# Hypergraph layer beside a state-space layer: norm chain, row norms and edge sums issued in separate, later steps

## The chip, the cores and the metric

The kernel runs on one core of a Trainium2 chip. Time is device time in microseconds (us). Engines are named as in the profile: PE does matmuls (PEld its weight loads), DVE is the vector engine, ACT the scalar engine, POOL is GpSimd, SP issues most of the DMAs. SBUF is the on-chip memory of 128 partitions; PSUM holds what PE writes[...].

## The reference

Four layers act on four images of 128 channels and 64 x 64 = 4096 points. Layer 0 is a Mamba-like scan over the points. Layer 1 is a hypergraph convolution on the group-normalized result. Layers 2 and 3, linear attention and experts, are not touched by the change. Layer 1, for one image, with `xf` the points as 4096 rows of 128 numbers:

```python
sq = jnp.sum(xf * xf, axis=-1)
d2 = sq[:, :, None] + sq[:, None, :] - 2.0 * jnp.einsum('bic,bjc->bij', xf, xf)
incidence = (jnp.sqrt(jnp.maximum(d2, 0.0)) < 16.0)
xe = jnp.einsum('bnc,dc->bnd', xf, W_fc) + b_fc
edge = jnp.einsum('bve,bvc->bec', incidence, xe) / deg_e
vert = jnp.einsum('bve,bec->bvc', incidence, edge) / deg_v
out = vert + xf        # then batch norm and SiLU, added to the layer's input
```

Layer 0's core is `h = dA * h + (dt * x) * B` for 16 states of 256 channels, point after point, and `y = sum(h * C)`.

## The kernel before, in words

`layers01` writes layers 0 and 1 as two Python generators and interleaves them. `layer0` works in chunks of 512 points, 8 per image, with 16 states per chunk. A state is two half-steps: ACT takes two exponentials into a PSUM tile (`hs`, L303), DVE scans both channel halves (L309), copies the carry (L318) and multiplies by C (`ho`, L319), POOL multiplies the drive (`db`, L291) and adds up eight states (`ho_s`, L324 and L326), PE sums into `ps_y` (L347) once a chunk. SP loads the rows B and C for each state (`bt`, L287). An image has 256 half-steps. Layer 0 runs 12 half-steps ahead (`LAG`).

`layer1(b)` is one image of the hypergraph. Its steps are: a prologue that turns the channel statistics of layer 0 into `rstd` and `nmr` (a matmul with `group` for the mean, `ps_gm`; a chain of one-column DVE operations L449 to L452; a second matmul `ps_gv`; a square root on ACT, L455; a reciprocal and a product on DVE), eight loads of `xn` and their normalization on ACT (L463); `tokens(q)`, which for 512 points takes squares on ACT (L468), their sums on PE (`ps_hc`), and `xe` with its split into two float16 parts in `xs`; then for each chunk c of 512 edges, from 7 down to 0, `compare` for the tiles up to c (PE `ps_g`, L504, and DVE `inc`, L507) and `turn` for the others, which gets them by transposing what is there (PE `ps_t`, L516, and ACT, L520). Rows of `inc` go to DRAM and come back as `strip` and `inc_v` by SP's queue. `row(c)` makes the row norm `hb` that `compare` of chunk c needs: a square on ACT, a matmul with ones (`ps_hb`, L495), a scaling on DVE (L497). `edges(inc, ed, c, i)` runs 32 matmuls into one PSUM tile (`ps_ed`, L527) that holds two parts of 129 columns each; ACT copies the first part to SBUF (L533) and DVE adds the second (L534). After four of them DVE, POOL and ACT divide by the degree and split `es` (L538 to L545). At the end, eight times, PE sums the vertices (`ps_v`, L627), `mean` scales on DVE (`rb`, L635) and adds `xn` on POOL (L636), and `finish` takes statistics on DVE (L639) and stores to DRAM (`hg`, L640).

The order comes from three things. `later(k, f)` puts a closure into `waiting`; `due()` runs it k ticks on. While layer 0 runs, a tick is one half-step of it. A planner gives each yield of `layer1` a weight (`W_CMP`, `W_EDGE` and so on) and, after each half-step, advances `layer1` until its share of the whole `work` is done. In the last image, with no layer 0 left, every yield is a tick. ACT's instructions are tied to the order in which they are written (`act`); the other engines' come from a scheduler that orders by priority and by when buffers come free.

The pools that matter: `ps` has four PSUM banks for all matmul results of both layers but `hs`; `tp` (squares and `xe` under one tag, `hb` and `dg`, `rb`, `inc`, `strip`) has two buffers for each tag; `xn` has one for each chunk.

```python
later(1, parts)     # in edges
later(1, mean)      # after the eighth group of vertex matmuls
later(4, finish)
```

Of the kernel before, what the change touches and what calls it, by code (L numbers as in the profile page):

```python
# [17 lines left out]
P = 128  # L18
# [23 lines left out]
class Net:  # L42
# [36 lines left out]
    def layers01(self):  # L79
# [6 lines left out]

        W_ROW, W_TOK, W_CMP, W_TURN, W_EDGE, W_LAST, W_DEG, W_VERT = 300, 450, 320, 75, 100, 630, 160, 267
        G = 8
        TO_POOL = (1, 4, 6, 9, 12, 14)
        LAG = 6 * 2  # L90
        with ExitStack() as ctx:
# [110 lines left out]
            def later(k, f):  # L202
                waiting.append((self.tick + k, f))
# [234 lines left out]

            def layer1(b):

                mv = tp.tile([P, 2], F32, tag="mv", name="mv")
                nc.vector.bn_aggr(mv, self.stats[:, b, :, :].rearrange("p c s -> p (c s)"))
# [4 lines left out]
                pg = ps.tile([P, CH], F32, tag="ps", name="ps_gm")  # L447
                nc.tensor.matmul(pg[:, :1], self.group, mv[:, 0:1], start=True, stop=True)
                nc.vector.tensor_copy(gm, pg[:, :1])  # L449
                nc.vector.tensor_tensor(nmr, mv[:, 0:1], gm, ALU.subtract)  # L450
                nc.vector.tensor_tensor(nmr, nmr, nmr, ALU.mult)
                nc.vector.tensor_tensor(nmr, nmr, mv[:, 1:2], ALU.add)  # L452
                pg = ps.tile([P, CH], F32, tag="ps", name="ps_gv")
                nc.tensor.matmul(pg[:, :1], self.group, nmr, start=True, stop=True)
                act(nc.scalar.activation(rstd, pg[:, :1], AF.Sqrt, bias=self.eps))  # L455
                nc.vector.reciprocal(rstd, rstd)
                nc.vector.scalar_tensor_tensor(nmr, gm, -1.0, rstd, ALU.mult, ALU.mult)

                xn = []
                for c in range(NCH):  # L460
                    x = wp.tile([P, CH], F32, tag=f"xn{c}", name="xn")
                    nc.sync.dma_start(x, self.x1[b][:, c * CH : (c + 1) * CH])
                    act(nc.scalar.activation(x, x, AF.Identity, scale=rstd, bias=nmr))  # L463
                    xn.append(x)

                def squares(c):
# [24 lines left out]

                def row(c):

                    ph = ps.tile([P, CH], F32, tag="ps", name="ps_hb")
                    nc.tensor.matmul(ph, self.ones, squares(c), start=True, stop=True)  # L495
                    hb = tp.tile([P, CH], F32, tag="hb", name="hb")
                    nc.vector.tensor_scalar(hb, ph, 0.5, -HALF, ALU.mult, ALU.add)  # L497
                    return hb

# [22 lines left out]
                def edges(inc, ed, c, i):  # L522
# [9 lines left out]
                    def parts():  # L532
                        act(nc.scalar.copy(ed[:, i, :], pe[:, : P + 1]))  # L533
                        nc.vector.tensor_tensor(ed[:, i, :], pe[:, P + 1 : 2 * P + 2], ed[:, i, :], ALU.add)  # L534
                        if i == 3:
# [10 lines left out]

                    later(1, parts)


                panels = [None] * NCH  # L550
                last = None
                hb = row(NCH - 1)
                yield W_ROW
                for c in range(NCH - 1, -2, -1):
# [6 lines left out]
                    for q in range(8):  # L561
                        if c == NCH - 1:
                            tokens(q)
                            yield W_TOK
                        if 0 <= c < q:
                            src = last[0][:, 4 * c : 4 * c + 4, :]
# [10 lines left out]
                        if c > 1:  # L577
# [5 lines left out]
                            )  # L583
                        if q == 6 and c > 0:
                            ahead = row(c - 1)
                            yield W_ROW
                        if last and q % 2:
# [3 lines left out]
                            yield W_EDGE if c >= 0 else W_LAST  # L591
                    hb = ahead
                    last = (inc, ed)
# [15 lines left out]
                for c in range(NCH):  # L609
# [39 lines left out]
            work = NCH * (W_ROW + W_TOK + W_DEG + 8 * W_VERT) + 4 * (NCH - 1) * W_EDGE + 4 * W_LAST  # L649
# [3 lines left out]
            for _ in range(states + LAG):  # L653
                next(l0)
            for b in range(B):
                l1 = layer1(b)
                if b < B - 1:
                    done = 0
                    for k in range(states):
                        next(l0, None)  # L660
                        self.tick += 1
                        due()
                        while done * states < work * (k + 1):
                            done += next(l1)
                else:
# [844 lines left out]
```

## Time and profile before

| | |
|---|---|
| median of 3 runs | 4132.1 us (4127.52 to 4135.44) |
| the profiled execution | 4130.31 us, span 4128.5 us |
| mean granted PE clock | 0.919 |
| busy share of the span | PE 84%, PEld 47%, DVE 72%, ACT 50%, POOL 60% |
| layer 0 of image 0 alone | to about 568 us |
| three passes, layer 0 of image b+1 beside layer 1 of image b | about 775, 775 and 763 us |
| layer 1 of image 3 alone | from about 2881 us |

The profile takes one execution with the hardware profiler. Its page lists busy time for each engine, the span in slices, the chain that ended last, and the costliest groups of instructions. Asked further, the trace lists who waited for whom, instructions in order of time, and busy time in chosen stretches. A wait is put down to what came last. In a line of a group or of the timeline, `out<-in` are the program's tile names, and the bracket or the last column tells how long the engine stood idle before it and what released it.

### The profile page before, as it was taken

How to read it: one execution, taken by the hardware profiler on the slowest of the kernel's cores; microseconds unless marked ns; L12 is line 12 of the kernel's file. 1: busy time of each engine (PE TensorE's matmuls, PEld its weight loads, DVE VectorE, ACT ScalarE, POOL GpSimd, SP SyncE). 2: the span in 40 equal slices, each digit the busy share in tenths (PEclk: the TensorE clock that was granted, in tenths of full speed). 3: DMA queues.
4: the chain of work that ended last, by engine and by line, in shares of the span. 5: the costliest groups of instructions: out<-in, count | busy, mean ns of one | idle time of the engine just before them, and what ended most of it. 6: DMA issues, size and time to landing. Idle time of an engine off the chain costs nothing. (4 is left out here: it accounts for less than half of the span.)

```text
span 4128.5 us, 48675 instructions
## 1 busy us (share of the span) xinstructions
PE 3469.8 (84%) x17243; PEld 1944.5 (47%) x17255; DVE 2990.9 (72%) x4628; ACT 2065.6 (50%) x3495; POOL 2460.4 (60%) x1242
## 2 busy tenths in 40 slices
PE   6878767888889688888977888888999979998999
PEld 2323323344543334445333344543566448765864
DVE  5888879999766799976669999765542057664874
ACT  4556554445644544555444445642124148852951
POOL 5999879888778788877869888775100020001300
PEclk8988977899999788999987899999999989999999
DMA  3445544555446344543644555447111330036138
GB/s 106 146 146 153 155 110 123 133 135 153 128 127 196 105 131 131 139 138 102 206 130 125 133 135 152 127 127 236 70 69 60 115 111 11 12 117 239 27 107 297
DMA packets 263847, 532.71 MB, mean 129 GB/s; under 512 B 22795, under 2 KB 25267, under 8 KB 262579
## 3 DMA queue, kind: packets, MB, share of 16 engines
q1 hardware_dynamic: 255666, 519.09, 43.1%
q10 hardware_dynamic: 7936, 10.52, 0.7%
q8 instruction: 136, 2.23, 0.2%
q14 instruction: 109, 0.89, 0.1%
HBM read 451.80 MB, written 77.73 MB: 128 GB/s over the span
## 5 line engine op out<-in xcount | busy, mean ns | idle before, releaser
L291 POOL TENSOR_TENSOR db<-dx,bt 128x1024 f32<-128x1024 f32 x512 | 1202.6, 2352 | 330.9 <-DVE hs L309 216.4
L309 DVE TENSOR_TENSOR_SCAN hs<-hs,carry,db 128x512 f32<-128x512 f32 x812 | 1037.2, 1285 | 174.6 <-ACT hs L303 91.8
L303 ACT ACTIVATE hs<-dl,A 128x512 f32<-128x512 f32 x1024 | 706.7, 692 | 750.2 <-DVE ho L319 696.8
L326 POOL TENSOR_TENSOR ho_s<-ho_s,ho 128x1024 f32<-128x1024 f32 x288 | 677.5, 2352 | 17.4 <-DVE ho L319 16.7
L504 PE MATMUL ps_g<-xn 128*128 128x512 f32 x1152 | 603.7, 654 | 99.8 <-DVE inc L507 74.8
L319 DVE TENSOR_TENSOR ho<-hs,bt 128x1024 f32<-128x1024 f32 x464 | 564.6, 1217 | 1.6
L527 PE MATMUL ps_ed<-xs,inc 128*128 128x258 f16 x4096 | 510.7, 285 | 19.1 <-ACT inc L520 8.6
L527 PEld LDWEIGHTS <-inc 128*128 128x128 fp8e4 x4096 | 416.3, 102 | 135.0 <-issue 62.4
L507 DVE SCALAR_TENSOR_TENSOR inc<-ps_g,hcl,hb 128x512 fp8e4<-128x512 f32 x576 | 422.0, 739 | 40.0 <-PE ps_g L504 24.4
L504 PEld LDWEIGHTS ps_g<-xn 128*128 128x128 f32 x1152 | 216.4, 205 | 417.5 <-DVE inc L507 184.1
L347 PE MATMUL ps_y<-ho,cst 128*128 128x512 f32 x512 | 276.3, 683 | 109.5 <-POOL ho L315 92.2
L627 PE MATMUL ps_v<-inc_v,es 128*128 128x512 fp8e4 x1536 | 342.9, 382 | 19.7 <-DVE rb L635 9.4
L627 PEld LDWEIGHTS <-es 128*128 128x128 f16 x2048 | 202.4, 99 | 289.5 <-issue 64.4
L520 ACT CAST inc<-ps_t 128x512 fp8e4<-128x512 f32 x448 | 232.2, 599 | 94.6 <-PE ps_t L516 94.6
L229 PE MATMUL ps_c<-xt,wc 128*128 128x512 f32 x512 | 231.3, 605 | 11.1 <-DVE inc L507 6.8
L347 PEld LDWEIGHTS ps_y<-ho,cst 128*128 128x128 f32 x512 | 106.2, 217 | 271.4 <-POOL ho L315 122.7
L533 ACT COPY ed<-ps_ed 128x129 f32<-128x129 f32 x128 | 34.1, 266 | 378.8 <-PE ps_ed L527 378.8
L534 DVE TENSOR_TENSOR ed<-ps_ed,ed 128x129 f32<-128x129 f32 x128 | 36.8, 288 | 211.2 <-ACT ed L533 208.1
L543 POOL TENSOR_TENSOR ed<-ed,rdeg 128x512 f32<-128x512 f32 x32 | 33.3, 1040 | 250.0 <-DVE rdeg L539 250.0
L1179 POOL CAST b1h<-b 128x512 bf16<-128x512 f32 x2 | 1.3, 649 | 299.7 <-DMA b<-in_L_ffn_weight 299.7
L309 DVE TENSOR_TENSOR_SCAN hs<-hs,db 128x512 f32<-128x512 f32 x116 | 141.4, 1225 | 52.9 <-POOL db L291 41.9
L229 PEld LDWEIGHTS ps_c<-xt,wc 128*128 128x128 f32 x512 | 98.2, 195 | 135.1 <-issue 115.9
(318 smaller groups left out, 5485.4 us busy)
## 6 DMA issues: line engine op xcount, KB each, us to landing
bt<-bcd SPq DMA_DIRECT2D x512, 512.0 KB, 5.1
w<-in_L_ffn_weight SPq DMA_DIRECT2D x64, 1024.0 KB, 11.4
inc<-inc SPq DMA_DIRECT2D x192, 256.0 KB, 2.8
inc_v<-inc SPq DMA_DIRECT2D x96, 512.0 KB, 6.3
strip<-inc SPq DMA_DIRECT2D x84, 256.0 KB, 4.8
x<-x ACTq DMA_DIRECT2D x32, 256.0 KB, 5.6
xn<-x SPq DMA_DIRECT2D x32, 256.0 KB, 5.6
hg<-rb SPq DMA_DIRECT2D x32, 256.0 KB, 2.6
```

The source lines that it names most:

```text
L229: nc.tensor.matmul(s["ps"][h], wc[:, h, j, :], xt[:, j : j + T], start=j == 0, stop=j == 3)
L291: nc.gpsimd.tensor_tensor(db, s["dx"], bc(s["bt", n][:, 0, :], 2), ALU.mult)
L303: act(nc.scalar.activation(hs[:, k, :], s["dl"][:, k, :], AF.Exp, scale=A[:, k, n : n + 1]))
L309: nc.vector.tensor_tensor_scan(to[:, h, :], hs[:, h, :], db[:, h, :], init, ALU.mult, ALU.add)
L319: nc.vector.tensor_tensor(ho, hs, ct, ALU.mult)
L326: nc.gpsimd.tensor_tensor(s["sum", n // G], s["sum", n // G], ho, ALU.add)
L347: nc.tensor.matmul(s["y"][h], self.ident, t[:, h, :], start=False, stop=n == DS - 1 and k == len(terms) - 1,)
L504: nc.tensor.matmul(pq, xn[v // 4][:, v % 4 * P : (v % 4 + 1) * P], xn[c], start=True, stop=True)
L507: nc.vector.scalar_tensor_tensor(inc[:, v, :], pq, hc[:, v : v + 1], hb, ALU.subtract, ALU.is_gt, saturate=False)
L520: later(1, lambda: act(nc.scalar.copy(inc[:, v, :], pt, saturate=False)))
L527: nc.tensor.matmul(pe[:, : 2 * P + 2], inc[:, v, i * P : (i + 1) * P], xs[:, v, :], start=v == 0, stop=v == NB - 1,)
L627: nc.tensor.matmul(pv, es[:, e, k, :], inc[:, e, :], start=e == 0 and k == 0, stop=e == NB - 1 and k == 1,)
```

## The change

- The prologue becomes a function of its own with four steps: means, variances, root, shift. The first three are written in the last three half-steps of layer 0 before the pass, the fourth at its start.
- `layer1` issues its eight `xn` loads in its first step. `normed(c)` normalizes chunk c and squares it. Chunk 7 and chunk 0 are done first; `tokens(q)` is given its squares, and `normed(q + 1)` is written behind it.
- `row(c)` is split into square, sum (2 ticks on) and scaling (3 ticks on), is written at q = 4 instead of 6 for all chunks but the first, and gives back a function that finishes what is left.
- `parts` adds both parts of an edge tile straight from PSUM with one DVE reduction over a view of 129 x 2, without ACT's copy, 2 ticks on instead of 1.
- `finish` comes 6 ticks on instead of 4.
- The planner's weights get `W_PRO` for the two new yields.

```diff
-            def layer1(b):
-                mv = tp.tile([P, 2], F32, tag="mv", name="mv")
-                nc.vector.bn_aggr(mv, ...)
...
+            def prologue(b):
...
+                def means():
+                    nc.vector.bn_aggr(mv, self.stats[:, b, :, :].rearrange("p c s -> p (c s)"))
+                    s["pg"] = ps.tile([P, CH], F32, tag="ps", name="ps_gm")
+                    nc.tensor.matmul(s["pg"][:, :1], self.group, mv[:, 0:1], start=True, stop=True)
+                def variances():
+                    nc.vector.tensor_copy(gm, s["pg"][:, :1])
...
+                def root():
+                    act(nc.scalar.activation(rstd, s["pg"][:, :1], AF.Sqrt, bias=self.eps))
+                def shift():
+                    nc.vector.reciprocal(rstd, rstd)
+                    nc.vector.scalar_tensor_tensor(nmr, gm, -1.0, rstd, ALU.mult, ALU.mult)
+                return rstd, nmr, [means, variances, root, shift]
+            def layer1(b, rstd, nmr):
                 for c in range(NCH):
                     x = wp.tile([P, CH], F32, tag=f"xn{c}", name="xn")
                     nc.sync.dma_start(x, self.x1[b][:, c * CH : (c + 1) * CH])
-                    act(nc.scalar.activation(x, x, AF.Identity, scale=rstd, bias=nmr))
                     xn.append(x)
+                yield W_PRO
...
+                def normed(c):
+                    act(nc.scalar.activation(xn[c], xn[c], AF.Identity, scale=rstd, bias=nmr))
+                    return squares(c)
-                def tokens(c):
-                    sq = squares(c)
+                def tokens(c, sq):
...
-                def row(c):
-                    ph = ps.tile([P, CH], F32, tag="ps", name="ps_hb")
-                    nc.tensor.matmul(ph, self.ones, squares(c), start=True, stop=True)
-                    hb = tp.tile([P, CH], F32, tag="hb", name="hb")
-                    nc.vector.tensor_scalar(hb, ph, 0.5, -HALF, ALU.mult, ALU.add)
-                    return hb
+                def row(c, sq=None):
...
+                    if sq is None:
+                        s["sq"] = squares(c)
+                        later(2, step)
+                        later(3, step)
+                    return get
...
                     def parts():
-                        act(nc.scalar.copy(ed[:, i, :], pe[:, : P + 1]))
-                        nc.vector.tensor_tensor(ed[:, i, :], pe[:, P + 1 : 2 * P + 2], ed[:, i, :], ALU.add)
+                        both = pe[:, : 2 * P + 2].rearrange("p (k c) -> p c k", k=2)
+                        nc.vector.reduce_sum(ed[:, i, :], both, axis=AX.X)
...
-                    later(1, parts)
+                    later(2, parts)
...
-                hb = row(NCH - 1)
-                yield W_ROW
+                hb = row(NCH - 1, normed(NCH - 1))
+                sq = normed(0)
+                yield W_PRO
...
-                            tokens(q)
+                            if q == 0:
+                                hb = hb()
+                            tokens(q, sq)
                             yield W_TOK
+                            if q < NCH - 2:
+                                sq = normed(q + 1)
+                            elif q == NCH - 2:
+                                sq = squares(q + 1)
...
-                        if q == 6 and c > 0:
+                        if q == (4 if c < NCH - 1 else 6) and c > 0:
                             ahead = row(c - 1)
...
-                    later(4, finish)
+                    later(6, finish)
```

More of the change, by code (lines that the diff above doesn't have):

```diff
@@ L84, in layers01 @@
         TOP = 2.0**14
-        W_ROW, W_TOK, W_CMP, W_TURN, W_EDGE, W_LAST, W_DEG, W_VERT = 300, 450, 320, 75, 100, 630, 160, 267
+        W_PRO, W_ROW, W_TOK, W_CMP, W_TURN, W_EDGE, W_LAST, W_DEG, W_VERT = 330, 300, 450, 320, 75, 100, 630, 160, 267
         G = 8
@@ L437, in layers01 @@
             stats = wp.tile([P, B, NCH, 6], F32, tag="stats1", name="stats1")
-            def layer1(b):
-                mv = tp.tile([P, 2], F32, tag="mv", name="mv")
-                nc.vector.bn_aggr(mv, self.stats[:, b, :, :].rearrange("p c s -> p (c s)"))
+            def prologue(b):
                 gm = tp.tile([P, 1], F32, tag="gm", name="gm")
@@ L446, in layer1 @@
                 nmr = tp.tile([P, 1], F32, tag="nmr", name="nmr")
[L447 to L457, printed above, removed]
+                mv = tp.tile([P, 2], F32, tag="mv", name="mv")
+                s = {}
+                def means():
[4 more added lines that the diff above has]
+                    nc.vector.tensor_copy(gm, s["pg"][:, :1])
+                    nc.vector.tensor_tensor(nmr, mv[:, 0:1], gm, ALU.subtract)
+                    nc.vector.tensor_tensor(nmr, nmr, nmr, ALU.mult)
+                    nc.vector.tensor_tensor(nmr, nmr, mv[:, 1:2], ALU.add)
+                    s["pg"] = ps.tile([P, CH], F32, tag="ps", name="ps_gv")
+                    nc.tensor.matmul(s["pg"][:, :1], self.group, nmr, start=True, stop=True)
+                def root():
[5 more added lines that the diff above has]
+            def layer1(b, rstd, nmr):
                 xn = []
@@ L490, in tokens, with sums, half, step @@
                     later(3, lambda: nc.gpsimd.tensor_tensor(lo, xe, hi, ALU.subtract))
-                def row(c):
-                    ph = ps.tile([P, CH], F32, tag="ps", name="ps_hb")
-                    nc.tensor.matmul(ph, self.ones, squares(c), start=True, stop=True)
-                    hb = tp.tile([P, CH], F32, tag="hb", name="hb")
-                    nc.vector.tensor_scalar(hb, ph, 0.5, -HALF, ALU.mult, ALU.add)
-                    return hb
+                def row(c, sq=None):
+                    s = dict(sq=sq)
+                    def sums():
+                        s["ph"] = ps.tile([P, CH], F32, tag="ps", name="ps_hb")
+                        nc.tensor.matmul(s["ph"], self.ones, s["sq"], start=True, stop=True)
+                    def half():
+                        s["hb"] = tp.tile([P, CH], F32, tag="hb", name="hb")
+                        nc.vector.tensor_scalar(s["hb"], s["ph"], 0.5, -HALF, ALU.mult, ALU.add)
+                    steps = [sums, half]
+                    def step():
+                        if steps:
+                            steps.pop(0)()
+                    def get():
+                        while steps:
+                            step()
+                        return s["hb"]
+                    if sq is None:
[3 more added lines that the diff above has]
+                    return get
                 def compare(inc, hb, c, v):
@@ L591, in layer1 @@
                             yield W_EDGE if c >= 0 else W_LAST
-                    hb = ahead
+                    if c > 0:
+                        hb = ahead()
                     last = (inc, ed)
@@ L643, in layer1 @@
                     later(1, mean)
-                    later(4, finish)
+                    later(6, finish)
                 while waiting:
                     due(True)
-            work = NCH * (W_ROW + W_TOK + W_DEG + 8 * W_VERT) + 4 * (NCH - 1) * W_EDGE + 4 * W_LAST
+            work = 2 * W_PRO - W_ROW + NCH * (W_ROW + W_TOK + W_DEG + 8 * W_VERT) + 4 * (NCH - 1) * W_EDGE + 4 * W_LAST
             work += NCH * (NCH + 1) // 2 * 4 * W_CMP + NCH * (NCH - 1) // 2 * 4 * W_TURN
@@ L652, in layers01 @@
             l0 = layer0()
-            for _ in range(states + LAG):
+            norm = prologue(0)
+            for k in range(states + LAG):
                 next(l0)
+                if k >= states + LAG - 3:
+                    norm[2].pop(0)()
             for b in range(B):
-                l1 = layer1(b)
+                norm[2].pop(0)()
+                l1 = layer1(b, *norm[:2])
                 if b < B - 1:
+                    norm = prologue(b + 1)
                     done = 0
@@ L664, in layers01 @@
                             done += next(l1)
+                        if k >= states - 3:
+                            norm[2].pop(0)()
                 else:
```

## The prediction

> **What bounds the kernel now.** The page gives PE 84%, DVE 72%, POOL 60%, averages over unlike stages. I cut the span into stages by busy time. Layer 0 of image 0 runs alone to 568 us, three passes (layer 0 of image b+1 beside the hypergraph of image b) run to 2881, the hypergraph of image 3 runs alone to about 3200, and the rest is untouched. Columns: length, then busy us of PE, PE weight loads, DVE, ACT, POOL, then granted clock, DMA share, GB/s. The first four rows are one pass: norm, compares, turns with edges, vertices.
>
> ```profile
> 568.00:595.00 27.00, 7.64 (x24) 5.92 (x25) 16.88 (x22) 16.44 (x23) 16.12 (x7) 0.50 0.30 78
> 595.00:1015.00 420.00, 350.20 (x1302) 176.98 (x1301) 388.57 (x499) 214.29 (x317) 371.44 (x169) 0.89 0.50 132
> 1015.00:1165.00 150.00, 127.02 (x847) 83.29 (x845) 100.80 (x128) 92.02 (x158) 104.55 (x49) 0.93 0.42 115
> 1165.00:1345.00 180.00, 157.68 (x620) 68.97 (x618) 123.04 (x127) 79.00 (x129) 147.42 (x69) 0.93 0.63 183
> ...
> 2881.00:3190.00 309.00, 279.58 (x1719) 184.30 (x1717) 132.55 (x214) 82.79 (x169) 23.24 (x21) 0.96 0.21 77
> ```
>
> No engine is full in a pass. DVE leads in the compares (31 us idle of 420), PE in turns and vertices (23 of 150 and 22 of 180 idle). So a DVE wait is worth about its length in the compares, and no more than PE's own idle time later. The last row is PE's. Next, the list of waits of DVE over the three passes: total us, times, longest.
>
> ```profile
> DVE stats L639 <- POOL rb L636: 103.7, 21, 8.9
> DVE hs L309 <- ACT hs L303: 101.3, 51, 5.2
> DVE ed L534 <- ACT ed L533: 75.8, 30, 7.8
> DVE hb L497 <- PE ps_hb L495: 59.8, 15, 8.6
> DVE hs L309 <- POOL db L291: 36.2, 32, 1.9
> ```
>
> The first, third and fourth are aimed at. The second hangs on them: ACT works in order, so an edge copy that waits for PE holds the exponentials of layer 0 behind it. Last, the timeline at the first prologue:
>
> ```profile
> 577.24 0.58 PE L454 MATMUL ps_gv<-nmr,cst 128*128 128x1 f32 x2 [8.58 <-DVE nmr L452]
> 577.86 0.26 ACT L455 ACTIVATE rstd<-ps_gv,eps 128x1 f32<-128x1 f32 x1 [3.36 <-PE ps_gv L454]
> ...
> 582.07 5.75 ACT L463 ACTIVATE xn<-xn,nmr,rstd 128x512 f32<-128x512 f32 x8 [3.94 <-DVE nmr L457]
> 587.85 1.15 ACT L468 ACTIVATE sq<-xn 128x512 f32<-128x512 f32 x2
> 588.53 0.50 PEld L495 LDWEIGHTS ps_hb<-sq,ones 128*128 128x128 f32 x2 [10.79 <-ACT sq L468]
> ...
> 590.64 0.69 DVE L497 TENSOR_SCALAR hb<-ps_hb 128x512 f32<-128x512 f32 x1 [8.61 <-PE ps_hb L495]
> ```
>
> Eight normalizations stand between the shift and the first square; PE and DVE wait for all of them. Layer 0's exponentials are queued behind.
>
> **What the Trainium skill says.** "VectorE: DVE Perf Modes" (The perf-mode tier table) has `tensor_reduce` in its 1x form alone. The trace agrees: 278 ns for 128 elements read and 553 for 384 is 1.07 ns an element. "SBUF — State Buffer" (SBUF: two separate sides) says a DVE operation with two SBUF inputs and a GpSimd operation exclude each other for a whole instruction. It agrees: the one-column `nmr` steps of L450 to L452 took 1.12, 1.18 and 2.26 us beside POOL's. Spreading the chain doesn't make them cheap. "TensorE: Matmul & The Clock Gate" (Part 1) has the clock fall after idle windows: 0.50 in the first row against 0.89 after it.
>
> **The change part by part.** The order of instructions in the two built programs tells what moves.
>
> *Prologue, four times.* The chain is emitted in the last three half-steps before the pass, but on DVE in passes 2 and 3 it stands back to back, with no scan between. What does change: the reciprocal now follows the variance directly (PE 0.58, ACT 0.26, about 1 us of wait as at the second prologue before), and ACT does normed(7), its square, normed(0), its square, not eight normalizations first. First pass: root ends 578.1; table load 1.28 and two exponentials 1.42 make 580.8; one normalization 0.80 and one square 0.63 make 582.2; PE's row sum 2.08 makes 584.3 for `hb` in place of 590.6: 6.3 gained with the same DVE work ahead of it. In passes 2 and 3 a new wait appears: chunk 7 is wanted first now, and its buffer is the last to come free, by the old pass's `rb` on POOL. I put that at 1350.5, the load at 2.4 to 5.6 us (a store of `rb` of that size lands in 2.4, these loads in the median in 5.6), normalization, square and sum at 3.5: `hb` at 1357 to 1360 against 1365.5. I take 7 each. In the last pass chunk 7 lands after the reloads as now, one normalization fewer follows it: 0.8. Sum 6.3 + 14 + 0.8 = 21.
>
> *Edges.* The 128 ACT copies of 266 ns go, and with them a link. In place of the 288 ns addition comes a reduction that reads 258 elements from PSUM: 292 (L1279, 128 elements) + 130 x 1.07 = 431 ns, an estimate, 0.14 more, 31 times in a pass's two middle stages: 4.4 us. A strided PSUM read isn't shown; bounds 290 (as cheap as the addition) and 580 (twice the elements, twice the time), so 0 to 9 us a pass; a gain is excluded, since it reads twice as many numbers from PSUM. It stands a tick later (about 3 us), so PE has mostly finished. Its bank, one of the four of `ps`, is held for that tick as well.
>
> *Row norms.* Square, sum and `hb` are a tick or two apart, and from the second chunk on the square is called two values of q sooner. The two buffers that squares and `xe` share alternate as before. `hb` waits of 11.4 in the middle stages go. PE's 12.5 us of waits for token squares go too; PE isn't the leader there, so I count 2 through `inc`'s waits.
>
> *Compares stage:* ed 4.7, hs behind ACT 3.1, hb 5.6 and that 2, less 17 x 0.14 = 2.4: 13. Other waits (POOL `db`, 7.5) take up some: 9 a pass. *Turns stage:* ed 20.5, hs 18.2, hb 5.8 less 14 x 0.14 make 42.5 of DVE, but PE has only 23 idle, part of it waits for `inc` on ACT: 10 a pass, bounds 0 and 23.
>
> *Finish two ticks later.* This aims at the 104 us of stats waits. Yet in both programs `stats` stands on DVE right behind its `rb` operation (one place a pass has a product between): the delay isn't in the order. The last `stats` of a pass, with four steps of the norm chain between before, now stands directly behind too; that wait is in the 1350.5 and what follows it above. POOL's `rb`, and SP's stores of `rb` and loads of `inc_v`, `bt` and `xn`, keep their places around it too. Taken at zero; if it did act, PE's 22 idle a pass is the ceiling.
>
> *Last pass alone.* PE waits 23.2 us for squares in six places, 14.0 at the start (counted above). The other 9.2 go: 9. The longer reduction lies beside PE, which is 95% busy there (279.58 - 3.61 of the 289 us from 2901 on).
>
> ACT's table loads go from 98 to 95 before exponentials, 4 us on an engine half idle: nothing. The weights of the planner rise by 360 of 84168: nothing.
>
> Sum: 21 + 3 x (9 + 10) + 9 = 87. The profiled execution took 4130.3 (span 4128.5), 1.8 under the median of 4132.1. So 4130.3 - 87 = 4043; I say 4045.
>
> **The rivals.**
> *PE and POOL take it up.* In a pass POOL is busy 637 of 775 and PE 640; coupled in-order engines could fill DVE's freed time with waits for `db` and for PSUM. Then only the prologue and the last pass pay: 21 + 9 = 30, 4100. For it: POOL waits in turn for DVE 71 us a pass, so all lean on each other. Against: beside layer 0 alone POOL ran at 91% (183 of the 200 us from 100 on), so it can do more than its 82% in a pass. 0.20.
> *All of PE's idle converts.* 13 + 23 a pass, warm clock included: 3 x 36 + 30 = 138, 3992; with some of the vertex stage too, 3960. 0.15.
> *The finish order acts after all.* It belongs to the last case's 3960.
> *Slower: the held bank.* PE already waits 46 us in three passes on banks held for `ed` (ps_t 21.6, ps_g 19.5, ps_y 4.4, ps_ed 0.9). A tick more on 93 edge groups of the passes, if PE stood still for all of it, is 93 x 3 = 279 us. It outweighs the 87 from about 0.95 us a group on. Against: three banks stay in turn, and PE has other matmuls between most edge groups. At 1.3 us a group 121 are lost and 87 won: 4165. 0.05.
> *Nothing nets.* Gains and new waits cancel, 4130. 0.02.
>
> **How the numbers follow.** The forecast case holds 0.58 (4020 to 4075). A difference under 0.2%, 8 us, can't be told from no change here. The range leaves out under half of the big case and the slower and null ones: 3985 to 4107. Faster by over 0.2%: 0.58 + 0.20 + 0.15 = 0.93; same 0.02; slower 0.05.
>
> **What would show it.** Right: no ACT copy of `ed`; `hb` waits on DVE in the passes down from 59.8 to under 25, most of it at the prologues for chunk 7's load; `ed` waits (now on PE) under 30; the reduction near 430 ns; stats waits still near 100; the pass from 775 to about 750; the last pass about 10 shorter. Wrong: a pass as long as before with longer waits for `db` or PSUM banks (first rival); stats waits gone; PE waits for `ed` above 100 (slower case).

## The result, and the profile after

The changed kernel takes 4104.9 us (median of four, 4101.2 to 4105.7) against 4133.8 before (4127.5 to 4135.5): a ratio of 0.9931, interval [0.9914, 0.9948]. It is faster, by 29 us. The forecast was 4045, a gain of 87: a third of it came.

Where it came from is read off stamps in the two traces: the first `hb` of each pass, the last `rb` that DVE takes in a pass, and the `bn` statistics that close the hypergraph of image 3.

| stretch | before, us | after, us | gain | forecast |
|---|---|---|---|---|
| start to first `hb` | 590.6 | 583.6 | 7.1 | 6.3 |
| last `rb` to next `hb`, passes 2, 3 | 16.4, 16.4 | 9.5, 9.5 | 13.8 | 14 |
| the same, last pass | 18.9 | 19.4 | -0.5 | 0.8 |
| first `hb` to last `rb`, three passes | 758.4, 758.4, 741.7 | 760.1, 755.2, 740.5 | 2.7 | 57 |
| `hb` to `bn`, last pass alone | 437.9 | 432.0 | 5.9 | 9 |

The sum is 29.1, the difference of the medians 28.9. That the two agree so closely is chance: the profiled spans differ by 24.6 only, as the untouched layers after `bn` took 794.2 us in the profile after and 789.7 before. So the prologue paid what was forecast, the last pass two thirds, and the three passes nearly nothing.

The stages in the profile after, cut like those of before; columns: length, then busy us of PE, PE weight loads, DVE, ACT, POOL, then granted clock, DMA share, GB/s.

```profile
567.00:590.00 23.00, 9.94 (x27) 6.62 (x28) 19.05 (x22) 13.04 (x18) 17.88 (x9) 0.50 0.31 90
590.00:1010.00 420.00, 350.07 (x1306) 175.08 (x1305) 393.81 (x503) 216.27 (x306) 376.21 (x171) 0.90 0.49 134
1010.00:1160.00 150.00, 125.86 (x848) 83.27 (x847) 98.65 (x124) 87.85 (x143) 102.15 (x48) 0.93 0.40 117
1160.00:1338.00 178.00, 155.13 (x597) 67.13 (x594) 120.23 (x123) 73.62 (x122) 140.16 (x66) 0.92 0.59 175
```

The first cut is made earlier, as `hb` comes 7 us sooner. The next two rows have the shape of before: DVE has 26 us idle of 420 in the compares (31 before), PE 24 of 150 in the turns (23 before). The list of waits of DVE over the passes (us in total, times, longest) says why DVE got no further:

```profile
DVE hs L309 <- ACT hs L303: 180.9, 66, 9.4
DVE stats L684 <- POOL rb L681: 107.9, 24, 8.9
DVE hb L518 <- PE ps_hb L514: 33.4, 6, 16.5
DVE ed L571 <- PE ps_ed L564: 30.2, 18, 3.4
DVE hs L309 <- POOL db L291: 24.5, 26, 1.9
```

Two of the three waits that were aimed at shrank: `ed` from 75.8 to 30.2, `hb` from 59.8 to 33.4, of which 16.5 is one wait at the last prologue. The waits of `stats` stayed, as the forecast had it. But waits for layer 0's exponentials rose by about as much as those two fell, from 101.3 to 180.9, and the longest from 5.2 to 9.4. They come from ACT, so its waits are the next view; first the kernel before:

```profile
ACT ed L533 <- PE ps_ed L527: 216.4, 75, 8.3
ACT inc L520 <- PE ps_t L516: 75.9, 39, 6.0
ACT es L544 <- POOL ed L543: 35.5, 12, 4.7
```

and the kernel after:

```profile
ACT inc L557 <- PE ps_t L553: 142.4, 52, 6.1
ACT es L581 <- POOL ed L580: 129.3, 23, 10.0
```

The wait of the edge copies, 216.4, is gone with the copies. 160 us came back on the two next kinds of instruction in ACT's order: the copies of turned tiles (+66.5) and the casts of `es` (+93.8), the latter with single waits of up to 10 us. Layer 0's own copies of `ps_xd` wait longer as well, 64.7 us instead of 40.5.

The prologue, by contrast, went as forecast. The timeline of the first one:

```profile
576.73 0.26 ACT L461 ACTIVATE rstd<-ps_gv,eps 128x1 f32<-128x1 f32 x1 [6.10 <-PE ps_gv L458]
...
579.66 0.80 ACT L485 ACTIVATE xn<-xn,nmr,rstd 128x512 f32<-128x512 f32 x1
...
580.49 0.63 ACT L480 ACTIVATE sq<-xn 128x512 f32<-128x512 f32 x1
...
581.17 2.08 PE L514 MATMUL ps_hb<-sq,ones 128*128 128x512 f32 x2 [4.47 <-ACT sq L480]
...
583.57 0.68 DVE L518 TENSOR_SCALAR hb<-ps_hb 128x512 f32<-128x512 f32 x1
```

One normalization and one square stand ahead of the row sum, not eight and one, and DVE no longer waits at `hb`: 583.6, where the forecast had 584.3.

### The profile page after: what moved, and what is told of

It is laid out like the page before. It is cut to its first block, busy times and chain, and to the rows that moved or that the text cites. A ratio compares the mean times of both kernels' runs of the same rounds, so it can differ in the third digit from the quotient of the medians.

```text
span 4103.9 us, 48550 instructions
## 1 busy us (share of the span) xinstructions
PE 3456.7 (84%) x17255; PEld 1931.4 (47%) x17255; DVE 3001.7 (73%) x4628; ACT 2034.9 (50%) x3364; POOL 2460.4 (60%) x1242
## 5 line engine op out<-in xcount | busy, mean ns | idle before, releaser
L544 DVE SCALAR_TENSOR_TENSOR inc<-ps_g,hcl,hb 128x512 fp8e4<-128x512 f32 x576 | 418.6, 735 | 26.3 <-PE ps_g L541 12.6
L571 DVE TENSOR_REDUCE ed<-ps_ed 128x129 f32<-128x258 f32 x128 | 52.9, 413 | 159.5 <-PE ps_ed L564 159.5
```

The costliest lines, as they stand in the source:

```text
L544: nc.vector.scalar_tensor_tensor(inc[:, v, :], pq, hc[:, v : v + 1], hb, ALU.subtract, ALU.is_gt, saturate=False)
```

## The experiments

"Passes" is the sum of the three stretches from a pass's first `hb` to its last `rb`, "last" the stretch from the last pass's `hb` to `bn`, both from the profiles. Each profile is one execution, and executions of one kernel spread by up to 20 us (4 us for `nr_load`, 13 us for `finish4`, 20 us for the kernel before), so a difference of a few us in these two columns is not shown. Ratios are to the kernel before, timed beside each.

| kernel | median us | ratio, interval | passes | last |
|---|---|---|---|---|
| before | 4131 to 4134 | | 2258.5 | 437.9 |
| changed | 4104.9 | 0.9931 [0.9914, 0.9948] | 2255.8 | 432.0 |
| only_norm | 4118.3 | 0.9967 [0.9956, 0.9978] | 2263.4 | 438.4 |
| only_rows | 4098.7 | 0.9922 [0.9909, 0.9935] | 2228.6 | 433.0 |
| only_edges | 4158.7 | 1.0066 [1.0051, 1.0081] | 2283.8 | 436.1 |
| norm_rows | 4089.0 | 0.9899 [0.9885, 0.9912] | 2239.3 | 433.1 |
| es_late | 4098.6 | 0.9922 [0.9907, 0.9936] | 2253.0 | 432.3 |
| parts1 | 4113.3 | 0.9955 [0.9942, 0.9967] | 2267.1 | 432.3 |
| copy2 | 4142.3 | 1.0027 [1.0017, 1.0036] | 2293.7 | 432.6 |
| add_twice | 4093.1 | 0.9904 [0.9889, 0.9919] | 2239.1 | 435.1 |
| parts1_copy | 4095.9 | 0.9911 [0.9896, 0.9926] | 2245.7 | 432.8 |
| exp_half | 4110.7 | 0.9954 [0.9942, 0.9967] | 2239.2 | 432.5 |
| exp_full | 4132.7 | 1.0001 [0.9993, 1.0009] | 2270.7 | 431.8 |
| exp_pass | 4088.0 | 0.9897 [0.9880, 0.9913] | 2236.5 | 431.3 |
| nr_exp | 4134.4 | 1.0010 [1.0002, 1.0018] | 2267.6 | 432.9 |
| pieces | 4092.0 | 0.9903 [0.9887, 0.9919] | 2253.0 | 420.9 |
| nr_load | 4081.3 | 0.9880 [0.9867, 0.9894] | 2237.9 | 433.2 |
| best | 4073.7 | 0.9858 [0.9843, 0.9873] | 2238.9 | 423.1 |
| finish4 | 4110.0 | 0.9954 [0.9940, 0.9968] | 2265.6 | 432.5 |
| best_exp | 4067.7 | 0.9847 [0.9833, 0.9860] | 2239.1 | 419.7 |

### Which part pays: only_norm, only_rows, only_edges, norm_rows

Each takes one part of the change into the kernel before; `norm_rows` is the changed kernel without its edges. For the edges:

```
# only_edges: before, with
-                        act(nc.scalar.copy(ed[:, i, :], pe[:, : P + 1]))
-                        nc.vector.tensor_tensor(ed[:, i, :], pe[:, P + 1 : 2 * P + 2], ed[:, i, :], ALU.add)
+                        both = pe[:, : 2 * P + 2].rearrange("p (k c) -> p c k", k=2)
+                        nc.vector.reduce_sum(ed[:, i, :], both, axis=AX.X)
-                    later(1, parts)
+                    later(2, parts)
# only_rows: before, with the new row(c), hb = ahead(), and
-                        if q == 6 and c > 0:
+                        if q == (4 if c < NCH - 1 else 6) and c > 0:
# only_norm: before, with prologue(b), normed(c), tokens(c, sq)
# norm_rows: the changed kernel, with the first edit undone
```

only_norm: 

> The kernel before with the prologue alone: norm's chain in steps, two normalizations ahead of the first row norm, the others and the token squares a chunk ahead. Row norms, edges and the finish as before. From the times of the first hb in the two traces: 7.1 us gained in the first pass, 5.5 and 5.3 in the next two, 4.1 lost in the last: 13.8, and up to 5 us in the last pass through the token squares. Theory B (the rest of the pass nets to nothing) expects 4115-4121, a gain of 13 to 19. Theory C (the parts give more alone than together, since each fills the same idle time) expects over 25 us, under 4109. The slip at the start of the last pass (chunks 6 and 7 land behind the reloads) should be here as well.

only_rows: 

> The kernel before with the row norms alone: squares, sum and hb a tick or two apart, from the second chunk on issued at the fifth value of q in place of the seventh. DVE's hb waits outside the prologues (11 us a pass) and PE's waits for row squares in the last pass go. The forecast had 2 x 5.7 us a pass; if other waits take them up, only the last pass pays, under 6 us. Theory B: 4120-4132; Theory C: a gain over 15 us, under 4119.

only_edges: 

> The kernel before with the edges alone: the reduction from PSUM two ticks later, without the ACT copy. The forecast had 20 to 25 us a pass of ed and exponential waits here, 4060-4075. Theory A and B expect little: ACT's waits for ps_ed (216 us) go and those for turned tiles and for POOL's ed at the es casts grow by over 120 us; DVE's waits for exponentials rise from 101 to over 150; 4115-4135. Theory C expects over 15 us of gain.

norm_rows: 

> The changed kernel with the edges as before (ACT copy and DVE addition one tick later); norm's steps, row norms in steps and the later finish stay. Alone, the edges cost 26 us, the norm part gained 14.4, the row norms 34. If the parts add, the time is 4132.7 - 14.4 - 34 = 4084, a pass 5.2 + 10.5 us under 775, about 759; if norm's part and the row norms fill the same idle time, 4090 or more. Either way clearly under 4105, if it is the edges that took the changed kernel's gain.

Measured: norm's part gained 14.4 us, where theory B had it, and the row norms 34.0. The edges lost 26.0, slower than any of the theories allowed. Without the edges the change takes 4089.0, 16 us less than with them. (The 4.1 us lost at the last prologue in the first expectation were counted from the norm's first matmul, which the changed kernel issues ahead of the last `rb`; counted from that `rb` it is 0.5.)

Theory C, that each part fills the same idle time, holds for the first two to a small degree: 14.4 + 34.0 = 48.4 apart, 43.2 together. For the row norms the size came, 2258.5 - 2228.6 = 29.9 in three passes and 4.9 in the last, but only part of it by the forecast's road, the 11.4 us of `hb` waits a pass. The waits of DVE in `only_rows`, from 568 to 2881 us as in the forecast's list:

```profile
DVE hs L309 <- ACT hs L303: 122.6, 54, 5.4
DVE ed L555 <- ACT ed L554: 62.1, 30, 5.1
DVE hb L502 <- PE ps_hb L498: 59.4, 10, 15.0
```

Of the 59.4 us at `hb`, 40.8 lie at the four prologues, which this run leaves as they were. (In the kernel before only three of them lie in this stretch, 25.8 of 59.8.) Within the passes `hb` waits went from 34.0 to 18.6, not to nothing. The waits for `ed` fell by 13.7, which the forecast had not counted here, and those for exponentials rose by 21.3. DVE was busy 9.5 us less, 5.1 of it in the degree step (`rdeg`, a DVE operation on four columns after each chunk's edges).

The edges are the part whose sign was wrong: 25.3 us lost in the passes alone, and 2255.8 - 2239.3 = 16.5 in company. The clock is not the reason: in the passes PE was busy 1891.0 us in the changed kernel and 1892.1 in `norm_rows`, and idle 364.8 and 347.2. What the edges cost is waiting.

### What in the edges costs: es_late, parts1, copy2, add_twice, parts1_copy

```
# es_late: changed, with
-                            later(3, lambda: act(nc.scalar.copy(hi, e)))
-                            later(4, lambda: nc.gpsimd.tensor_tensor(lo, e, hi, ALU.subtract))
+                            later(6, ...)   and   later(7, ...)
# parts1: changed, with
-                    later(2, parts)
+                    later(1, parts)
# copy2: changed, with the ACT copy and the DVE addition back, later(2, parts) kept
# add_twice: norm_rows, with one more addition ahead of the real one
+                        again = tp.tile([P, P + 1], F32, tag="again", name="again")
+                        nc.vector.tensor_tensor(again, pe[:, P + 1 : 2 * P + 2], ed[:, i, :], ALU.add)
# parts1_copy: parts1, with the old copy ahead of the reduction, into a tile that nothing reads
+                        spare = tp.tile([P, P + 1], F32, tag="spare", name="spare")
+                        act(nc.scalar.copy(spare, pe[:, : P + 1]))
```

es_late: 

> The changed kernel with one edit: the casts of es on ACT six ticks after a chunk's edges in place of three, the low halves on POOL seven in place of four. Theory A (the blocked time moved to es): in the changed kernel's passes ACT waits 129 us for POOL's scaled ed at these casts (35 before), and layer 0's exponentials queue behind them. Then the wait should fall under 40, DVE's waits for exponentials (181 us) should fall by 40 to 60, and the time should fall from 4105 to 4050-4070. Theory B (ACT waits for whatever comes next in its order, and PE's edge groups set it): the es wait goes, ACT's waits for turned tiles (142 us) grow, DVE's waits for exponentials stay within 20 us of 181, and the time stays within 8 us of 4105.

It took 6 us less than the changed kernel, with overlapping intervals. The casts' waits fell from 129.3 to 32.2, but those for turned tiles stayed (146.9) and DVE's for exponentials fell by 6 only. Theory A, that the casts alone are the matter and can be cured by moving them, fell.

parts1: 

> The changed kernel with one edit: the reduction from PSUM one tick after its edges in place of two. Theory D (the delay costs: the chunk's last part, and with it POOL's scaling and the es casts, comes a tick later and falls on PE and ACT at a worse place) expects 4075-4090. Theory E (without the copy ACT runs on into turned tiles and es casts and waits there; and the reduction is 0.14 us longer than the addition) expects 4100-4115, DVE's waits for ps_ed from 30 back to over 60.

copy2: 

> The changed kernel with the ACT copy and the DVE addition back, but two ticks after the edges: the delay without the reduction. Theory D expects 4100-4115, as slow as the changed kernel or slower; Theory E expects 4080-4092, ACT's waits for ps_ed well under the 216 us of before, and its waits for turned tiles near the 76 of before.

Neither theory fits both. The delay with the old copy costs 53 us over `norm_rows`; the reduction without the delay costs 24; both together 16. So it is neither the delay nor the reduction as such, and the parts don't add. Two runs then took one suspected cost each.

add_twice: 

> norm_rows (4089; edges by ACT copy and DVE addition) with each addition done twice, the first into a spare tile that nothing reads: 0.28 us more of DVE for each of 128 edge groups, 96 of them in the passes, 27 us, and nothing else. If DVE's time in the passes is paid in full (theory I), the time is 4110-4118, and the 0.125 us that the reduction takes longer explains 12 of the 16 to 24 us that it cost. If DVE's time there hides in its waits (theory J: ACT's order is what costs), 4086-4098.

```profile
L573 DVE TENSOR_TENSOR ed<-ps_ed,ed 128x129 f32<-128x129 f32 x128 | 36.9, 288 | 3.4
L572 DVE TENSOR_TENSOR again<-ps_ed,ed 128x129 f32<-128x129 f32 x128 | 36.7, 287 | 207.3 <-ACT ed L570 207.2
```

These are rows of its groups of instructions (total us, mean ns of one, then idle time before them and what ended it). 36.7 us of DVE were added, 27.5 of them in the passes, and the passes took 2239.1 us against 2239.3. The time rose by 4.1, of which 2.0 lie in the last pass. Theory I, that DVE's time in the passes is paid in full, fell.

parts1_copy: 

> The changed kernel with the reduction one tick after its edges (4113) and, ahead of it in ACT's order, the old ACT copy again, into a spare tile that nothing reads: ACT waits for PE at each edge group as before, DVE has the longer reduction without the link from ACT. Theory J (the copy's wait kept ACT from running into longer waits further on) expects 4085-4098 and ACT's waits for es casts back under 60. Theory I expects 4105-4120: the reduction's time on DVE is still there.

It took 4095.9, 17 us less than `parts1`, although ACT does 128 more copies whose result nobody reads, and DVE's reductions wait for them. Waits of ACT in `parts1`, over the passes:

```profile
ACT inc L557 <- PE ps_t L553: 144.8, 57, 7.5
ACT es L581 <- POOL ed L580: 142.3, 24, 10.2
```

and in `parts1_copy`:

```profile
ACT spare L571 <- PE ps_ed L564: 217.1, 71, 8.3
ACT es L583 <- POOL ed L582: 44.5, 12, 5.2
ACT inc L557 <- PE ps_t L553: 33.3, 19, 4.2
```

The three kinds sum to 287 and 295: about the same, at other places. Layer 0's copies of `ps_xd` add 66.3 in `parts1` and 29.7 here. DVE's waits for exponentials are 157.7 in `parts1` and 109.3 here.

`parts1_copy` still takes 6.9 us more than `norm_rows`, 6.4 of it in the passes. The two have the same order on PE and ACT and nearly the same on DVE; what is left is the reduction, 0.13 us longer than the addition. So the longer reduction is a small part of the cost. Why it costs anything where `add_twice`'s additions cost nothing stays open.

How can an idle copy make a kernel faster? The order of instructions in the two programs gives an answer, though by elimination. On PE the two are the same, instruction by instruction; on ACT they are the same but for the copies, save that a few DMA issues stand a place off. "Perfetto Trace Analysis" of the Trainium skill (Tensor Engine Instruction (MATMUL, LD_WEIGHTS)) has ACT, DVE and GpSimd work strictly first in, first out; nothing in these traces contradicts it. As long as every instruction takes the same time, taking a copy out then can't by itself make anything later. What differs is the place of the reductions on DVE, which the scheduler chooses: in `parts1` 30 of 128 stand one to three scans later than in `parts1_copy`, 6 a scan sooner; 12 of the 32 degree steps that follow a chunk's last reduction stand two scans later; 12 of POOL's 32 scalings of `ed` stand behind one to three more of layer 0's operations. A few DMA issues of SP trade places as well. With the copy in place, the reductions' order is that of `norm_rows` for 125 of 128. The `es` casts keep their places on ACT. One such chunk, in the timeline of `parts1` (second pass, the last edge group of chunk 7):

```profile
1547.71 3.74 PE L564 MATMUL ps_ed<-xs,inc 128*128 128x258 f16 x32
...
1551.08 2.61 DVE L309 TENSOR_TENSOR_SCAN hs<-hs,carry,db 128x512 f32<-128x512 f32 x2
...
1553.59 0.40 DVE L571 TENSOR_REDUCE ed<-ps_ed 128x129 f32<-128x258 f32 x1
...
1558.02 2.36 POOL L271 TENSOR_TENSOR dl<-dl,sp 128x1024 f32<-128x1024 f32 x1
...
1562.77 1.04 POOL L580 TENSOR_TENSOR ed<-ed,rdeg 128x512 f32<-128x512 f32 x1
...
1563.84 0.62 ACT L581 CAST es<-ed 128x512 f16<-128x512 f32 x1 [7.68 <-POOL ed L580]
...
1565.88 1.29 DVE L309 TENSOR_TENSOR_SCAN hs<-hs,carry,db 128x512 f32<-128x512 f32 x1 [2.05 <-ACT hs L303]
```

and the same chunk in `parts1_copy`:

```profile
1542.21 0.27 ACT L571 COPY spare<-ps_ed 128x129 f32<-128x129 f32 x1 [2.75 <-PE ps_ed L564]
...
1542.51 0.42 DVE L573 TENSOR_REDUCE ed<-ps_ed 128x129 f32<-128x258 f32 x1 [0.63 <-ACT spare L571]
...
1546.43 1.04 POOL L582 TENSOR_TENSOR ed<-ed,rdeg 128x512 f32<-128x512 f32 x1
...
1547.43 2.35 POOL L271 TENSOR_TENSOR dl<-dl,sp 128x1024 f32<-128x1024 f32 x1
...
1549.81 0.60 ACT L583 CAST es<-ed 128x512 f16<-128x512 f32 x1
```

In `parts1` the reduction stands behind two scans of layer 0 though PE is done at about 1551.5; POOL's scaling then falls behind `dl` and the product after it and comes 15 us after the edge matmuls began, not 8 (they began at 1538.43 in `parts1_copy`); ACT stands 7.7 us at the cast, and DVE's next scan waits 2.05 us for the exponentials behind it.

A place changes durations too: the 24 degree steps of the passes took 44.4 us together in `parts1` and 28.9 in `parts1_copy`, 15.5 us of DVE on the way to the casts. Which of these places and durations cost how much was not tried one by one, and no run fixed DVE's order alone.

The changed kernel against `norm_rows` shows the same shift: 51 of 128 reductions stand one to three scans later and 6 one sooner, 12 of 32 degree steps two scans later, and 15 of POOL's scalings one to four operations later, while 23 of 32 `es` casts keep their place among the exponentials on ACT. (The degree steps took 27.2 and 27.6 us there, so they are no part of that loss.) The other runs that lost show it too: 51 of 128 later in `only_edges` than before, 66 in `copy2` than in `norm_rows`. But a later place is not a loss by itself: in `exp_half`, below, 42 stand later than in the changed kernel, and its passes are faster.

### ACT's order by itself: exp_half, exp_full, nr_exp, exp_pass

If ACT's order ahead of the exponentials is what costs, they can be moved instead of the rest.

```
# exp_half: changed, with the exponentials taken out of state(s, n, 0) into exps(s, n), and in layer0
+                    if i + 1 < count:
+                        exps(*at(i + 1))
                     state(*at(i), 1)
# exp_full: the same lines ahead of state(*at(i), 0)
# nr_exp: nr_load (below) with exp_half's edit
# exp_pass: exp_half from the second image on: if NT * DS <= i + 1 < count
```

exp_half: 

> The changed kernel with one edit outside the change: the two exponentials of a layer 0 state stand half a state earlier in ACT's order (ahead of the copies that fall due in the second half of the state before), the buffers as before. Theory F: what costs is that ACT, in order, stands at turned tiles (94 us of DVE's 181 us of waits for exponentials have that ahead of them in the trace) and at es casts (63) just ahead of exponentials that DVE wants at once. Then DVE's waits for exponentials fall from 181 to under 110, and the time from 4105 to 4050-4080. Theory G: PE is what everything waits for in the turns, and the exponentials' waits only show it: they fall, but waits for ps_ed, ps_hb and db on DVE grow, and the time stays within 10 us of 4105.

exp_full: 

> The changed kernel with the exponentials a whole state earlier in ACT's order, as early as their two buffers allow. Theory F expects still fewer waits for exponentials, under 70 us, and 4040-4075, unless ACT's own waits for DVE's ho, now ahead of the copies, keep PE's banks: then PE's waits for inc grow. Theory G expects 4095-4115.

nr_exp: 

> The best version so far (edges as before, norm and row norms in steps, xn loads ahead of the reloads: 4081) with the exponentials half a state earlier. There, 74 of DVE's 113 us of waits for exponentials have ACT's edge copies ahead of them. Theory F expects 4050-4070. Theory G 4075-4090.

exp_pass: 

> The changed kernel with the exponentials half a state earlier in ACT's order from the second image on; layer 0 of the first image, alone, as it was. In the run with them earlier everywhere the passes took 16 us less than in the changed kernel's profile and layer 0 alone 24 more. If both hold, 4085-4093; if the passes' gain depended on the order that came before them, 4100-4110.

`exp_half` was a miss for theory F: 4110.7. Its profile parts two effects: the passes took 16.6 us less than the changed kernel's, and layer 0 of the first image alone 24.6 more (first `hb` at 608.2, not 583.6). `exp_pass` leaves the first image as it was, and both held: 4088.0, passes of 2236.5, DVE's waits for exponentials down from 180.9:

```profile
DVE hs L311 <- ACT hs L296: 127.2, 52, 7.5
```

So half a state earlier in ACT's order, from the second image on, is worth 17 us to the changed kernel, as much as taking its edges out. Theory F has the direction, not the size: it asked for waits under 110 and at least 25 us. Some waits moved on again, as theory G has it, those for `ps_ed` from 30.2 to 39.1.

A whole state earlier loses 28 us (4132.7), 14 of them in layer 0 alone and 15 in the passes; PE's waits for ACT's copies of turned tiles (`inc`) went from 39.4 to 53.3, the exception that theory F named.

The half with the edges as before loses 53 (`nr_exp` against `nr_load`), 24 of them again in layer 0 alone and 30 in the passes. Of the 30, 14.4 are PE's busy time, at a granted clock of 0.905 instead of 0.920, and 15.2 its idle time; 45 of the 128 additions stand one or two scans later. What causes what there stays open. Theory F is no general rule.

### The last pass: pieces, nr_load, best, best_exp; and the finish

```
# pieces: changed, with each group of 32 edge matmuls as four of 8, one after each turned tile or compare that follows
# nr_load: norm_rows, with the first step of the last layer1 (the xn loads) ahead of the reloads
+                    next(l1)
                     only0.close()
                     self.reload()
# best: nr_load, with pieces in the last pass only
# best_exp: changed, with exp_pass, nr_load's edit, and pieces in the last pass only
# finish4: changed, with
-                    later(6, finish)
+                    later(4, finish)
```

pieces: 

> The changed kernel with each group of 32 edge matmuls (3.7 us of PE in one go) cut into four of 8 that stand between the turned tiles or compares that follow; the reduction two ticks after the last. Theory H: ACT's waits for turned tiles come from PE doing an edge group ahead of them. They fall from 142 us in the passes to under 80, DVE's waits for exponentials from 181 to under 140, and the time to 4065-4090. If they don't fall, it isn't the group's length, and the time stays at 4095-4115; the bank of an edge group is held longer, which may cost up to 1 us a group, 4180 at worst.

The waits for turned tiles fell to 126.9 only and the passes by 2.8: theory H fell there. The last pass, where layer 0 is gone, took 11.0 us less. Stage rows of it, the changed kernel first:

```profile
2878.00:3173.00 295.00, 285.35 (x1808) 190.16 (x1809) 134.41 (x211) 77.77 (x146) 24.07 (x22) 0.99 0.17 62
```

```profile
2877.00:3161.00 284.00, 280.53 (x1815) 187.68 (x1816) 134.82 (x211) 81.38 (x146) 24.13 (x22) 0.99 0.18 65
```

Over nearly the same matmuls PE's idle time went from 9.7 to 3.5 us and its busy time from 285.4 to 280.5. The profile models the ends of matmuls, so the split between busy and idle is less sure than the sum of 11 us.

nr_load: 

> norm_rows with one edit more: in the last pass the eight loads of xn are issued ahead of the reloads of the batch norm's inputs in place of behind them. In the changed kernel chunk 7 landed 17 us after ACT began to wait for it there, since its load stood behind the reloads. If that is what lost 4.1 us at the last prologue, hb of the last pass comes 10 to 17 us sooner after its norm than in norm_rows, as PE has nothing else to do then, and the time falls by as much: 4068-4076. If instead chunk 7's buffer comes free late (by POOL's last addition), under 4 us.

The last prologue in the changed kernel, and below it in `nr_load` (ACT's wait for chunk 7, and `hb`):

```profile
2863.64 1.41 SPq L474 DMA_DIRECT2D xn<-x  x2
2874.11 0.81 ACT L485 ACTIVATE xn<-xn,nmr,rstd 128x512 f32<-128x512 f32 x1 [17.23 <-DMA xn<-x]
```

```profile
2843.64 0.43 SPq L474 DMA_DIRECT2D xn<-x  x1
2847.93 0.81 ACT L485 ACTIVATE xn<-xn,nmr,rstd 128x512 f32<-128x512 f32 x1 [8.30 <-DMA xn<-x]
```

Behind the reloads the load was used 10.5 us after its issue, ahead of the last five of them 4.3. From the last `rb` to `hb` it is 10.5 us in place of 17.7 in `norm_rows`, and the time fell by 7.6, less than the 10 to 17 expected.

best: 

> nr_load (4081; edges as before, norm and row norms in steps, xn loads ahead of the reloads) with the edge groups cut into four among the turned tiles in the last pass alone, where this took 11 us in the changed kernel and nothing in the passes: 4069-4073. If the cut pays only with the reduction from PSUM, 4078-4084.

best_exp: 

> The changed kernel with its own edges (reduction two ticks later) and three edits: exponentials half a state earlier from the second image on (17 us alone), the xn loads ahead of the reloads in the last pass (8 us on norm_rows), and edge groups in four among the turned tiles in the last pass (10 us alone or less): 4105 - 17 - 8 - 10 = 4070 if they add; 4078-4085 if the two in the last pass share one idle time. Against best (4074), which has the edges as before.

finish4: 

> The changed kernel with the finish of a vertex chunk four ticks after its product, as before, in place of six. The forecast costed this at nothing, since the stats stay right behind rb on DVE in either; SP's stores move by a place or two among its loads. Expected within 4 us of 4105, waits of stats for rb within 5 us of 108. If the finish had an effect of its own, over 8 us either way.

`best` took 4073.7; the cut of the edge groups pays with the old edges too (433.2 to 423.1). `best_exp` took 4067.7, 0.9847 of the kernel before, interval [0.9833, 0.9860]: the fastest here, with the reduction from PSUM in it; its three edits add up as expected (4070). `finish4` took 5.1 us more than the changed kernel: the two intervals just overlap, but each of its five runs is slower than each of the changed kernel's four. The stats waits are 107.5 there and 107.9 in the changed kernel. In its profile, a slow execution of that kernel (4116.7), the third pass alone took 9.1 us more, with PE busy 12.3 us longer and idle 3.1 less at a granted clock of 0.904 instead of 0.918. So the excess of that execution lies in PE's busy time and not in its waits. Whether the finish itself is worth a few us is not settled.

## Why the prediction was right or wrong

- **Prologue, 21.** Right: 20.4 by the stamps (7.1 + 13.8 - 0.5). The new wait for chunk 7's load at passes 2 and 3 came and was priced right. The last prologue gained nothing, for the load behind the reloads, as the working had it.
- **Row norms.** Right in size: 29.9 us in the passes when alone, 34 by the `hb` waits. The mechanism was right in part: those waits fell by 15.4, and the rest came through shorter `ed` waits and less busy time, less what the exponentials took back.
- **Edges: the step that failed.** "Compares stage: ed 4.7, hs behind ACT 3.1" and "turns stage: ed 20.5, hs 18.2" counted the exponentials' waits as a result of the edge copy, to go with it. The part was to gain and lost: 25.3 us in the passes alone, 16.5 in company. The `ed` waits did shrink, to 30.2. The exponentials' waits grew, since ACT's next waits, at turned tiles and at `es` casts, took the copy's place, and, by elimination, since the scheduler set part of the reductions, and what follows them, later. `parts1_copy` shows the link: with the copy back, order, waits and 17 us come back. How the loss splits over the places is not shown. 3 x (9 + 10) = 57 became 2.7: the row norms' 29.9, less the 4.9 that norm's part alone loses in the passes, and less 16.5 for the edges, would leave 8.5; the rest is lost between norm's part and the row norms, which together gain 5.8 less in the passes than apart. (These terms are from single executions, so the small ones are rough.) The forecast looked at what waited on DVE, and not at what stood behind the removed instruction in ACT's order. It asked what would be late next at the prologue, and found chunk 7's load; it did not ask this for `ed`.
- **The reduction, 431 ns.** 413 measured, which is 0.93 ns for each element beyond the 292 ns of 128. That fits the single 1x form which "VectorE: DVE Perf Modes" of the Trainium skill (The perf-mode tier table) has for it. Whether the 4.4 us a pass set against the gain were owed is not clear: `add_twice` added 27.5 us of DVE in the passes at no cost, while the reduction in the place of the addition cost 6.4 (`parts1_copy` against `norm_rows`).
- **Last pass, 9.** Mis-sized: 5.9. PE's waits for row squares there went from 9.2 to 4.8, not to nothing. PE was idle 4.0 us less there; the other 2.0 are its busy time, 417.4 to 415.4, at a granted clock of 0.98 and 0.99.
- **Finish, nothing.** Upheld for the waits: stats still wait 107.9 us. Whether the time was untouched is open: `finish4` took 5.1 us more.
- **Rivals.** "PE and POOL take it up" gave 4100 and the place (prologue and last pass pay, 30), and both came: 4104.9 and 26.3. Its mechanism didn't: DVE's waits for `db` fell from 36.2 to 24.5. It was ACT that took it up, so that rival's number was luck. The held bank was refuted: PE's waits on banks held for `ed` went from 46 to 29 us.
- **The stated signs.** No ACT copy, the reduction's length and the stats waits were right. `hb` waits of 33.4 are under 25 only without the last prologue (16.9), and `ed` waits of 30.2 just missed 30. The pass "from 775 to about 750" was the one that told: its three stretches were 2.7 us shorter in all.

## What to carry to other kernels

Before counting the wait of a removed instruction as a gain, list what stands behind it in its engine's order and what each of those waits for: the time moves to the first of them that isn't ready, and only what is no longer waited for at the instruction that the leading engine wants (here the exponentials) is a gain. Where a scheduler places the other engines' instructions, compare their order in the two programs as well: here an edit to one engine moved part of another's work by a whole state. Change parts of such an edit one at a time, since here two of three paid 43 us together and the third gave 16 of them back.

## What was not expected of the hardware

- A reduction of two strided halves straight from PSUM (128x129 out of 128x258) took 413 ns, less than in proportion to the 288 ns of the addition that reads one half from SBUF.
- DVE operations on four columns were among its dearest for their size. The degree step after each chunk, in the changed kernel's groups:

```profile
L575 DVE TENSOR_SCALAR rdeg<-ed 128x4 f32<-128x4 f32 x32 | 28.5, 891 | 0.4
```

  In single cases it took from 0.2 to 2.2 us, while the reciprocal right after it on the same four columns took 0.14 to 0.18 each time. "SBUF — State Buffer" of the Trainium skill (Who interferes with whom) counts this kind among those that can contend with GpSimd for a shared pair of ports, for a whole instruction; POOL's products here take 2.35 us, which fits, though no run took POOL away to prove it.
- Cutting PE's 3.7 us edge groups in four among other matmuls shortened its busy time by 4.9 us in 285, beside the idle time that it saved.
